# A two-layer convolution and feed-forward block: W_up moved to SyncE's queue, convolution 1 ahead of pair 3's first layer, eight weight sums moved to GpSimd

## The chip, the cores and the metric

One core of a Trainium2 chip runs the whole program once. Its engines are TensorE (PE, with PEld for its weight loads), VectorE (DVE), ScalarE (ACT), GpSimd (POOL) and SyncE (SP, which here only issues DMAs). Every engine works through its own instructions in the order in which the program has them, and waits on semaphores for the others. The metric is the device time of one launch in microseconds (us); the median over runs counts. All data is float32.

## The reference

`x` is 128 sequences of 64 channels and 1024 positions. Two layers follow each other, each a convolution-like step and then a matrix product over the 1024 positions, added to `x`:

```python
# layer 0: a 64x64 channel mix per sequence, chosen by attention over 8 kernels,
# then a product of rank 128
att   = softmax(gelu(gelu(cond @ W0 + b0) @ W1 + b1) @ W2 + b2)
agg_w = einsum('bk,koi->boi', att, weight)
out   = einsum('boi,bih->boh', agg_w, x) + (att @ bias_k)[:, :, None]
x     = x + einsum('bsd,od->bso', out, A @ B.T) + bias
# layer 1: a grouped convolution (4 groups, 9 taps), plus a context per sequence,
# then a full 1024x1024 product and a routed low-rank part
y     = conv1d(x, weight1, groups=4, padding=4) + (c @ c_weight.T)[:, :, None] + bias1[None, :, None]
delta = lora_B[e] @ (lora_A[e] @ y)         # e = argmax(gate_w @ y + expert_bias)
x     = x + y @ W_up.T + delta
```

## The kernel before

**Tiles.** Two sequences make a pair: 128 rows (two sequences of 64 channels) by 1024 positions, 0.5 MB. There are 64 pairs, numbered from 0. Two pairs make a step of the outer loop (L784), 32 steps in all. Constants such as W_up (4 MB, tile `w`), `at`, `bt`, `ws` stay in SBUF.

**Layer 0 of one pair** is three functions. `layer0_in` (L387) multiplies the turned x (`xt`) by B: 16 PE instructions into `pxb`, one ScalarE copy to `xb`. `layer0_mix` (L396) mixes channels with the pair's own 128x128 matrix into `pz`, and copies to `z`. The first four pairs (`FIRST = 4`) build that matrix on VectorE from their attention row (`own_bd`, L325, eight operations, tile `bdx`) and a bias on ScalarE (`own_bias`, L319, tile `mv`). Later pairs take it from DRAM, where `agg_all` and `agg_out` put all sequences' matrices (`aggd`, 2 MB), read back as `bd` and `ab` by `load_cond` (L232). `layer0_out` (L412) multiplies by A in two halves into `pd`; VectorE adds each half into `x` (L423), and SyncE writes it to a DRAM scratch `x1d` (L424) and reads it back in another layout as `X` (L431, L432), which waits until the write has landed. With `later=True` the two reads are returned as a function and issued where that is called. Before `layer0_out` the feed-forward bias must have been added to `x` (`add_fbias`, L646).

**Layer 1.** For the first two pairs (`PLAIN = 2`) the convolution `conv` (L524) multiplies `X` by `ws` directly: 64 PE instructions at L496 into `pc`; VectorE adds the context into `yt` (L517). Later pairs use differences of `X` built by GpSimd (`differences`, L451, tile `df`), a shared product `pm` (L467) added by VectorE (L482) and copied by ScalarE (L485), then L505 into `pc`, and L517.

**The 1024x1024 product** of a step is done as a fast block scheme: sums of quarters of `yt` (`Y_SUMS`, on GpSimd, `ffn_sums`, tiles `s`), sums of blocks of W_up (`W_SUMS`, once, `w_sums`), and 26 products of four PE instructions each (`PRODUCTS`, L549, into `pb`), whose results are added into place by VectorE and ScalarE. There are 31 entries in `W_SUMS`; each is one operation on 128x512 in the tile `w`. In `w_sums` ScalarE first copies one of the two operands to PSUM (`pw`, L197), and VectorE then adds (L206 or L204), except where an operand is one of the last two results, which is read from SBUF as it is. `gate_in`, `gate` and `turn` make the routed part's choice.

**The prologue** (L680 to L783) is ordered by hand over all five engines; every list below is in program order. SyncE: the loads of pairs 0 and 2, then for pairs 0 and 1 the writes and reads of `layer0_out`, with pair 3's loads (L705) between them, and pair 4's loads (L718) behind pair 1's reads; then the writes of pairs 2 and 3, their reads, the aggregated matrices, `load_cond(2)`, pair 5. ScalarE's queue: pair 1's loads and several constants, `gl` and `lb` (L715, L716), and the four quarters of W_up (L724, `load_w`, in the order 2, 1, 3, 0) between its own copies. The first 26 products come in `first_products` (L749), which before product i issues the sums that product i + 3 needs. The sums 0 to 2 are issued ahead of all products by `w_sums(3, False)`, with both operands in SBUF. DMAs issued by SyncE and ScalarE share eight completion semaphores taken in turn, so an issue can wait for the landing of the one eight places before it.

## Time and profile before

| | us |
|---|---|
| median of 3 runs | 1291.03 (1288.48 to 1291.08) |
| the profiled execution: its time | 1288.22 |
| its span | 1286.4 |
| PE busy in the span | 1259.9 (98%) |
| GpSimd / VectorE / ScalarE busy | 721.8 / 705.0 / 237.0 |
| first product (L549) starts | 57.8 |
| `pd` of pair 4 / of pair 5 starts | 80.3 / 87.1 |
| `pm` of pair 4 (L467) starts | 104.2 |
| X of pair 1: reads issued / landed | 33.4 and 34.2 / 47.5 and 49.2 |
| DMA over the span | 189.71 MB, mean 147 GB/s |

### The profile page before, as it was taken

How to read it: one execution, taken by the hardware profiler on the slowest of the kernel's cores; microseconds unless marked ns; L12 is line 12 of the kernel's file. 1: busy time of each engine (PE TensorE's matmuls, PEld its weight loads, DVE VectorE, ACT ScalarE, POOL GpSimd, SP SyncE). 2: the span in 40 equal slices, each digit the busy share in tenths (PEclk: the TensorE clock that was granted, in tenths of full speed). 3: DMA queues.
4: the chain of work that ended last, by engine and by line, in shares of the span. 5: the costliest groups of instructions: out<-in, count | busy, mean ns of one | idle time of the engine just before them, and what ended most of it. 6: DMA issues, size and time to landing. Idle time of an engine off the chain costs nothing.

```text
span 1286.4 us, 23722 instructions
## 1 busy us (share of the span) xinstructions
PE 1259.9 (98%) x9255; PEld 1059.1 (82%) x9255; DVE 705.0 (55%) x1484; ACT 237.0 (18%) x593; POOL 721.8 (56%) x861
## 2 busy tenths in 40 slices
PE   8789999999999999999999999999999999999998
PEld 6567888888888888888888888888888888888886
DVE  6586554555554565554565454565454565455454
ACT  2242112111112111111111111111111111111111
POOL 2345764556765546765556765546765555765432
PEclk9899999999999999999999999999999999999999
DMA  9954446544446544445654445654445654445301
GB/s 310 312 164 134 124 110 175 175 149 141 127 110 173 174 148 143 133 106 169 175 155 138 130 110 166 174 156 141 131 110 162 175 162 132 133 115 157 103 34 66
DMA packets 184158, 189.71 MB, mean 147 GB/s; under 512 B 17392, under 2 KB 156656, under 8 KB 183536
## 3 DMA queue, kind: packets, MB, share of 16 engines
q1 hardware_dynamic: 166192, 121.61, 34.7%
q0 software_dynamic: 16128, 58.73, 13.6%
q10 hardware_dynamic: 1728, 7.87, 1.7%
q8 instruction: 74, 1.21, 0.4%
q14 instruction: 36, 0.29, 0.1%
HBM read 118.90 MB, written 69.27 MB: 146 GB/s over the span
## 4 chain that ended last, share of the span: by engine, by line
PE 93%; DMA 3%; DVE 2%; issue 0%; ACT 0%; SPq 0%; DVEq 0%
PE pb L549 55%; PE pxb L391 9%; PE pd L422 8%; PE pc L505 8%; PE pm L467 5%; PE pg L576 4%; PE pb L622 3%; DMA X<-x1d 1%; PE pz L401 1%; DMA x<-in_x 1%; DVE yt L517 1%; DMA x1d<-x 1%; DMA xt<-in_xt 0%; PE pc L496 0%; DVE m L482 0%
## 5 line engine op out<-in xcount | busy, mean ns | idle before, releaser
L549 PE MATMUL pb<-w,s 128*128 128x256 f32 x2432 | 556.9, 380 | 1.8 <-DVE pb L554 0.9
L549 PEld LDWEIGHTS pb<-w,s 128*128 128x128 f32 x2432 | 459.9, 190 | 68.5 <-issue 1.7
L459 POOL TENSOR_TENSOR df<-X 128x512 f32<-128x512 f32 x62 | 64.3, 1037 | 390.8 <-DMA X<-x1d 362.3
L549 PE MATMUL pb<-w,yt 128*128 128x256 f32 x896 | 226.2, 381 | 2.6 <-DVE x L628 1.8
L482 DVE TENSOR_TENSOR m<-pm,cx 64x512 f32<-64x512 f32 x124 | 85.5, 689 | 201.7 <-PE pm L467 198.8
L549 PEld LDWEIGHTS pb<-w,yt 128*128 128x128 f32 x896 | 163.1, 191 | 31.8 <-issue 8.7
L566 DVE TENSOR_TENSOR x<-pb,x 128x256 f32<-128x256 f32 x320 | 129.1, 420 | 94.8 <-PE pb L549 88.1
L206 POOL TENSOR_TENSOR s<-yt,s 128x256 f32<-128x256 f32 x224 | 164.0, 732 | 17.8 <-PE pb L549 2.8
L647 POOL TENSOR_TENSOR x<-x,ffn_bias 128x1024 f32<-128x1024 f32 x62 | 144.8, 2352 | 42.0 <-DMA x<-in_x 42.0
L391 PEld LDWEIGHTS pxb<-B,xt 128*128 128x128 f32 x1024 | 118.8, 194 | 25.6 <-DVE yt L517 22.0
L517 DVE TENSOR_TENSOR yt<-pc,m 128x512 f32<-128x512 f32 x124 | 122.1, 1108 | 22.2 <-ACT m L485 20.0
L422 PE MATMUL pd<-AT,z 128*128 128x512 f32 x256 | 122.6, 601 | 3.4 <-DVE attx L317 1.3
L391 PE MATMUL pxb<-B,xt 128*128 128x128 f32 x1024 | 124.9, 280 | 1.0 <-PE pb L549 0.9
L505 PE MATMUL pc<-ws,df 128*64 128x128 f32 x1984 | 114.0, 273 | 1.2 <-DVE m L482 1.2
L423 DVE TENSOR_TENSOR x<-pd,x 128x512 f32<-128x512 f32 x128 | 88.3, 691 | 44.7 <-PE pd L422 38.1
L505 PEld LDWEIGHTS pc<-ws,df 128*64 128x64 f32 x1984 | 109.4, 137 | 1.6 <-POOL s L206 1.0
L561 ACT COPY v<-pb 128x256 f32<-128x256 f32 x96 | 35.8, 372 | 372.9 <-PE pb L549 355.4
L206 POOL TENSOR_TENSOR s<-s,yt 128x256 f32<-128x256 f32 x128 | 93.4, 730 | 14.9 <-PE pzt L613 7.5
L485 ACT COPY m<-m 64x512 f32<-64x512 f32 x124 | 76.6, 617 | 135.5 <-DVE m L482 125.7
L206 POOL TENSOR_TENSOR s<-s,s 128x256 f32<-128x256 f32 x128 | 92.7, 735 | 5.0
L568 DVE SCALAR_TENSOR_TENSOR x<-pb,x 128x256 f32<-128x256 f32 x128 | 54.0, 422 | 68.2 <-PE pb L549 66.6
L628 DVE TENSOR_TENSOR x<-pb,x 128x512 f32<-128x512 f32 x124 | 76.7, 681 | 8.7 <-PE pb L622 8.7
(107 smaller groups left out, 919.3 us busy)
## 6 DMA issues: line engine op xcount, KB each, us to landing
x1d<-x SPq DMA_DIRECT2D x128, 256.0 KB, 4.5
X<-x1d SPq DMA_DIRECT2D x128, 256.0 KB, 4.3
out<-x SPq DMA_DIRECT2D x62, 512.0 KB, 3.6
xt<-in_xt POOLq DMA_DIRECT2D x56, 512.0 KB, 5.8
x<-in_x POOLq DMA_DIRECT2D x56, 512.0 KB, 6.6
cx<-ctxd SPq DMA_DIRECT2D x32, 128.0 KB, 4.2
w<-in_wq ACTq DMA_DIRECT2D x4, 1024.0 KB, 7.7
ab<-aggbd SPq DMA_DIRECT2D x30, 128.0 KB, 3.3
```

What stands on the lines that cost most here:

```text
L206: eng.tensor_tensor(to, x, y, ALU.add if op == "+" else ALU.subtract)
L391: nc.tensor.matmul(pxb[:, :P], xt[:, c, :], bt[:, c, :], start=(c == 0), stop=(c == NC - 1))
L422: nc.tensor.matmul(pd, z0, at[:, cols], start=True, stop=True)
L423: nc.vector.tensor_tensor(x[:, cols], pd, x[:, cols], ALU.add)
L482: nc.vector.tensor_tensor(by_group(m2[half, b]), by_group(pm[half]), context(pr, b, half), ALU.add)
L485: nc.scalar.copy(m2[other, b], m2[half, b])
L505: nc.tensor.matmul(pc[o * H : (o + 1) * H, cols], diffs[pr][:, 2 * g + b, o], ws[:, g, o], start=True, stop=True,)
L517: nc.vector.tensor_tensor(yt.rearrange("m q (o g two) -> m two g q o", two=2, g=NGC)[:, b], by_group(pcs.pop((pr, b))), context(pr, b) if ...
L549: nc.tensor.matmul(p, ys[d][u][:, c], W[:, w, c], start=new == 1 and c == 0, stop=c == QC - 1, skip_group_check=True)
L566: nc.vector.tensor_tensor(x, p, x, ALU.add)
L628: nc.vector.tensor_tensor(x[:, cols], b, x[:, cols], ALU.add)
L647: eng.tensor_tensor(xs[pr], xs[pr], fbias, ALU.add)
```

## The change

Nothing of what is computed changes, except that eight sums are done on another engine. In the prologue:

- **W_up** is issued by SyncE instead of ScalarE, behind pair 1's two reads of X and pair 4's turned x. `load_x` is split in two, so that pair 4's turned x goes ahead of W_up and pair 4's x behind it and behind pair 2's writes. `lb` moves from ScalarE's queue to SyncE's, behind that. Pair 3's loads move from between pair 0's reads and pair 1's writes to between pair 1's writes and reads.
- **Convolution 1** moves from behind `layer0_out(3)` to between `layer0_in(3)` and `layer0_mix(3)`. `layer0_in(4)` moves from the middle of the first eight products to ahead of the gates and products.
- **Eight sums** (`ON_POOL`: 16, 19, 20, 21, 23, 24, 27, 28 of `W_SUMS`) are done by GpSimd from SBUF, without ScalarE's copy.
- **Biases**: pair 3's goes from GpSimd to VectorE, behind pair 2's output; pair 4's, on GpSimd, from ahead of the first sums of `yt` to behind the last.
- `own_bias` of pairs 2 and 3 goes up beside that of pair 1; of the products around `layer0_mix(4)` and (5), some change places with the mixes and `layer0_in(5)`.

```diff
 NW = 26
+ON_POOL = (16, 19, 20, 21, 23, 24, 27, 28)
...
+    def load_turned(pr, eng):
+        xts[pr] = xtp.tile([P, NC, P], F32, tag="xt", name=f"xt{pr}")
+        eng.dma_start(xts[pr], a["xt"][pr])
+
+    def load_rest(pr, eng):
+        xs[pr] = xpool.tile([P, L], F32, tag="x", name=f"x{pr}")
+        eng.dma_start(xs[pr], a["x"][pr])
+
     def load_x(pr, eng=nc.gpsimd):
...
+        load_turned(pr, eng)
+        load_rest(pr, eng)
...
             first = W[:, x]
+            if k in ON_POOL:
+                combine(nc.gpsimd, W[:, to], first, op, W[:, y])
+                continue
             if aside and x not in fresh:
...
-    own_bias(1)
+    for pr in range(1, FIRST):
+        own_bias(pr)
     load_context(0)
     layer0_out(0)
 
-    load_x(3, nc.sync)
     add_fbias(1, nc.vector)
...
     gl = loaded("gl", [P, NC, GT], eng=nc.scalar)
-    lb = loaded("lb", [P, N], eng=nc.scalar)
-    layer0_out(1)
-    load_x(4, nc.sync)
+    back1 = layer0_out(1, later=True)
+    load_x(3, nc.sync)
+    back1()
+    load_turned(4, nc.sync)
+    for k in (2, 1, 3, 0):
+        load_w(k, nc.sync)
     wsum = const.tile([P, NGC, P], F32, tag="sel", name="wsum")
     nc.gpsimd.tensor_tensor(wsum, ws[:, :, 0], ws[:, :, 1], ALU.add)
-    add_fbias(3, nc.gpsimd)
     next(agg)
-    for k in (2, 1, 3, 0):
-        load_w(k, nc.scalar)
     own_bd(2)
-    own_bias(2)
     layer0_in(2)
     own_bd(3)
-    own_bias(3)
     conv(0)
     layer0_mix(2)
     back2 = layer0_out(2, later=True)
+    load_rest(4, nc.sync)
+    lb = loaded("lb", [P, N], eng=nc.sync)
+    add_fbias(3, nc.vector)
     layer0_in(3)
+    conv(1)
     layer0_mix(3)
     back3 = layer0_out(3, later=True)
     back2()
...
     w_sums(3, False)
-    conv(1)
+    layer0_in(4)
 
     gate_out(0, gate_in(0))
-    add_fbias(4, nc.gpsimd)
     ffn_sums(0, 0, 10)
...
-    first_products(4)
-    layer0_in(4)
-    first_products(4)
+    first_products(8)
     differences(2)
     differences(3)
     ffn_sums(0, 10)
+    add_fbias(4, nc.gpsimd)
     add_fbias(5, nc.gpsimd)
...
-    first_products(4)
+    first_products(3)
     layer0_mix(4)
+    first_products(1)
     layer0_out(4, lambda: load_x(6, nc.sync))
-    first_products(2)
     layer0_in(5)
+    first_products(1)
     layer0_mix(5)
+    first_products(1)
     layer0_out(5, lambda: load_x(7, nc.sync))
```

More of the change, by code (lines that the diff above doesn't have):

```diff
@@ L152, in block @@
     xs, xts, bds, aggbs, ctxs = {}, {}, {}, {}, {}
+    def load_turned(pr, eng):
[4 more added lines that the diff above has]
+        eng.dma_start(xs[pr], a["x"][pr])
     def load_x(pr, eng=nc.gpsimd):
-        xts[pr] = xtp.tile([P, NC, P], F32, tag="xt", name=f"xt{pr}")
-        xs[pr] = xpool.tile([P, L], F32, tag="x", name=f"x{pr}")
-        eng.dma_start(xts[pr], a["xt"][pr])
-        eng.dma_start(xs[pr], a["x"][pr])
+        load_turned(pr, eng)
+        load_rest(pr, eng)
     BD = []
```

## The prediction

> **What bounds the kernel now.** I read the stage table first, to see where TensorE is not full; then the chain of waits in the stage where it is not; then the DMA queues in the wait that the chain names; then the timeline of GpSimd and VectorE, since work moves between them. Pairs are counted from 0.

> In the stage table the columns are the stretch, its length, then busy time (and instructions) of PE, PEld, DVE, ACT and POOL, the granted clock, the DMA share and GB/s:

> ```profile
> 0.00:29.00 29.00, 23.66 (x127) 16.90 (x127) 18.63 (x46) 8.67 (x22) 6.54 (x20) 0.94 0.91 305
> 29.00:58.00 29.00, 20.36 (x193) 15.86 (x194) 14.87 (x23) 2.14 (x9) 6.71 (x5) 0.88 0.99 305
> 58.00:68.00 10.00, 9.14 (x52) 7.71 (x53) 8.10 (x14) 7.39 (x17) 9.53 (x13) 1.00 0.72 243
> 68.00:80.00 12.00, 9.83 (x114) 8.28 (x110) 11.81 (x20) 4.24 (x7) 7.57 (x8) 1.00 0.34 100
> 80.00:104.00 24.00, 20.76 (x84) 15.00 (x84) 17.50 (x36) 9.29 (x20) 10.75 (x9) 0.93 0.73 189
> 104.00:1286.00 1182.00, 1176.17 (x8692) 995.32 (x8690) 634.05 (x1348) 205.26 (x519) 680.66 (x809) 1.00 0.48 139
> ```

> From 104 us on, PE is busy 1176 of 1182 us: whatever brings that point forward ends the kernel earlier by as much. The change touches only what lies before it. Of 29 to 58 us PE works 20.4, with the DMA engines full (0.99). From 58 to 104 PE works 39.7 of 46, and VectorE is the fullest engine from 68 to 80 (11.8 of 12).

> The chain of waits between 20 and 60 us (start, length, what):

> ```profile
> 27.54 6.64 DMA x1d<-x
> ...
> 34.19 15.02 DMA X<-x1d
> ...
> 49.35 5.40 PE pc L496 x64
> ...
> 55.90 1.96 PE pg L576 x30
> ```

> Convolution 1 (L496) waits for pair 1's X, whose read takes 15.02 us; pair 0's took 5.6. The DMA view of 34 to 44 us says why:

> ```profile
> q10 hardware_dynamic: 471, 3.46, 94.3%
> q1 hardware_dynamic: 283, 0.14, 5.3%
> ```

> q10 is ScalarE's queue, on which W_up (4 MB) was issued from 31.0 us; q1 is SyncE's, with X. X moves 0.14 MB in 10 us beside W_up's 3.46.

> VectorE and GpSimd in the timeline (start, length):

> ```profile
> 30.72 4.64 DVE L332 SCALAR_TENSOR_TENSOR bdx<-wk,attx,bdx 128x128 f32<-128x128 f32 x7
> ...
> 32.40 2.42 POOL L647 TENSOR_TENSOR x<-x,ffn_bias 128x1024 f32<-128x1024 f32 x1 [8.53 <-DMA x<-in_x]
> ```

> The same seven VectorE operations took 2.68 us without GpSimd beside them: 1.96 more for GpSimd's 2.42. And later GpSimd stands idle for 16.4 us:

> ```profile
> 92.56 1.04 POOL L459 TENSOR_TENSOR df<-X 128x512 f32<-128x512 f32 x1 [16.44 <-PE pb L549]
> ```

> **W_up behind X.** Pair 1's sums are ready at 24.70 and 25.93 (L423); SyncE issues their writes then, no longer behind pair 3's loads. A write and a read take 4.5 + 4.3 at the page's medians, 6.6 + 5.6 in the loaded stretch: X is there between 34.8 and 38.2, not at 49.2. W_up follows in the queue behind pair 3's 1 MB, X and pair 4's turned x, from about 36. At q10's 3.46 MB in 10 us its 4.19 MB take 12.1: the last quarter lands near 49, 2 us later than before (47.1). The first sum that needs it is W_SUMS[3].

> **TensorE to product 0.** ScalarE no longer issues W_up, where it stood 7.2 us ahead of the copy that mix(2) waits for. Convolution 0 at 29.4, as before, takes 3.7: 33.1. Mix 2 x 0.49, copy 0.3, output 2.0: 36.4. L391 for pair 3, 2.0: 38.4. Convolution 1 (X is there by either bound), 3.7 by convolution 0's row; its own 5.4 came at a granted clock of 0.70 after an idle stretch that is gone: 42.1. Mix, copy and output of pair 3, 3.3: 45.3. L391 for pair 4 2.0, gates L576 1.9: product 0 at 49.2 against 57.8. VectorE keeps up: without pair 3's bias on GpSimd its second row of seven ends at 33.3, not 35.4. It takes that bias itself (1.23, the row at 12.9 us) at 37.2, ahead of the convolution's first half at 40.2; were pair 3's x to land after 39, the cover would be gone and all 1.23 would count. The four ScalarE activations moved up (0.29 each, 1.2) lie in its 3.05 us gap before 19.3; lb's issue moves to SyncE, where it costs 0.8 of waiting time.

> What is late next is VectorE: W_SUMS 0 to 2 now meet GpSimd's sums (0.73 each, from 43), which came after them before. Each 0.69 waits between 0 and 0.73; I take all: 46.1 + 4.3 = 50.4 when sum 3 starts, against 58.7. **Gain so far 8.3.** [...]

> **To the convolutions of pairs 2 and 3.** Sum 3 to L482 took 58.7 to 70.8, VectorE nearly without a gap. L391 for pair 4 (2.0 on PE) leaves it, but VectorE sets the pace: between 0 and 2.0, I take 0.5. X of pairs 2 and 3 must be there by 61. Their writes now queue behind W_up (to 48), then pair 4's x and lb (0.75 MB, 1.9 at the 400 GB/s of a full stretch): X lands near 55 and 58, hidden by 3 us.

> **The eight sums.** Each leaves VectorE (0.69) and ScalarE (0.59, its copy to PSUM) and costs GpSimd 1.04 by the row at 92.56 (same shape), or 2.12 by L720's, which ran against VectorE. I take 1.04, as VectorE's other sums read PSUM copies: 8.3 us inside an idle 16.4. Sum 16 stands behind bias 5, which waits for pair 5's x. Behind the sums wait differences 4, biases 6 and 7, differences 5: 74.7 + 8.3 + 2.1 + 4.7 + 2.1 = 91.9, wanted by L505 at 95.6, hidden by 3.7.
> From L482 to pd of pair 4: 9.6 before, one sum less: 0.6. From there to L467 at 104.2: 23.9 before. PE's own work in it is 14 products at 0.865 (chain: 16 matmuls 3.46), two outputs 3.5, L391 2.0, mix and wait 1.3, transposes 0.3: 19.2. So 4.7 at most, and nothing at least, if VectorE's dependent steps stay. Seven of the eight sums leave here (4.8 of VectorE's 17.5), so PE becomes the bound: I take 4.6.

> **Sum** 8.3 + 0.5 + 0.6 + 4.6 = 14.0. The profiled execution took 1288.2 (span 1286.4): 1274.2. The runs shown lie 0.3 to 2.9 above it, median 2.8; I add half: **1275.5**. The ends: no lock (0.8), X of pair 0 1 us sooner since lb is out of its way, 1.5 more in the second stage: 17.3, and 18 with the range's rounding; without the last stage 9.4.

> **Rivals.**
> A: *the aggregation's DMA chain becomes the bound.* The same bytes go through engines that were full to 64 us. From pair 3's last write (50.3) the chain ran 15.2 to agg, 4.9 to ab, 3.3 to pair 5's x (73.7). New it starts at 46.2 with 3 us of transfers ahead: ab near 69, x near 72.5, needed at 69.7 and 72.6. For: no slack. Against: only the excess counts. If nothing lands sooner than before, mix(4) waits 0.7 and sum 16 is up to 3 late: gain 10.5, 1279.
> B: *GpSimd at 2.12 a sum:* 17 us, differences 5 end 5 late: gain 9, 1280.5. Against: VectorE has few operations with two SBUF tiles there.
> C: *moving W_up does nothing for X,* which lands at 45 to 49 anyway, and pair 3's layer 0 stands behind a late convolution. For: the same bytes, full engines. Against: the 0.14 MB. Convolution 1 at 45.5 to 49.3 instead of 38.4 takes 7 to 11 of the 14: 1282 to 1287. [...]
> D, *slower: SyncE's head blocks.* X's reads wait on SyncE for the write's landing, and now W_up, the next writes and the aggregation stand behind them. Each us that X is late past 38.4 moves convolution 1 and W_up alike: even at 52.4, slower by over 0.2% from 55; at 58, 1294. For: SyncE stood 9.2 us ahead of pair 2's write, for a read of X that this write did not need. Against: it takes 29 us from write to read, and the 6.6 + 15.0 was with W_up on another queue.
> E: *no effect*, 1288 to 1291: only if PE's idle returned elsewhere in full.

> **Chances.** Forecast 0.62, A 0.15, B 0.06, C 0.09, D 0.05, E 0.03. The range runs from 18 of gain (1270) over A and B to the middle of C: 1270 to 1284. A measurement here tells 0.2% (2.6 us) from no change. Faster: all but D, E and the end of C, 0.91; same 0.04; slower 0.05.

> **What would show it.** Pair 1's X landing before 38.4, W_up's last near 49; convolution 1 before mix(3), from about 38; product 0 near 49; sums on GpSimd near 1.04, in a row from about 75; pair 4's first L467 near 90; the rest 1182 long. Wrong: X after 45, mix(4) waiting for ab, product 13 for GpSimd, or over 30 us from product 0 to pd of pair 5.

## The result, and the profile after

| | before | after |
|---|---|---|
| median on the same chips, 5 runs each | 1288.48 us (1284.06 to 1291.08) | 1278.93 us (1277.43 to 1279.74) |
| ratio of the means, 95% interval | | 0.9935 (0.9915 to 0.9954) |
| the profiled execution: time, span | 1288.22, 1286.4 | 1279.21, 1277.4 |

Faster by 0.65%: 9.0 us in the profiled spans, where the forecast had 14.0. Functions lie ten lines further down in the changed kernel: L496 is now L506, L549 L559, L423 L433, L424 L434, L467 L477, L482 L492, L595 L605, L647 L657. Points of the two traces beside the forecast, in us:

| | before | forecast | after |
|---|---|---|---|
| pair 1's X landed (two reads) | 47.5, 49.2 | 34.8 to 38.2 | 34.4, 36.0 |
| W_up's last quarter landed | 47.1 | 49 | 47.6 |
| convolution 1 starts | 49.4 | 38.4 | 37.2 |
| product 0 starts | 57.8 | 49.2 | 47.8 |
| first L482 (now L492) | 70.8 | 62.0 | 60.7 |
| `ab` landed; pair 5's x landed | 70.4; 73.7 | 69; 72.5 | 69.4; 72.0 |
| `pd` of pair 4 | 80.3 | 70.9 | 69.9 |
| `pm` of pair 4 | 104.2 | 90.2 | 95.5 |
| from there to the end | 1182.2 | 1182 | 1181.9 |

Up to pair 4's `pd` the change gave 10.4 us, 1.0 more than forecast (9.4). From there to pair 4's `pm` it lost: that stage took 23.9 before, 19.3 was forecast, and it takes 25.5. So 14.0 + 1.0 - 6.2 + 0.3 (the rest) gives the 9.0 within rounding. The stage table of the changed kernel shows the same; its columns are those of the table shown before:

```profile
29.00:48.00 19.00, 18.01 (x199) 14.37 (x194) 14.74 (x24) 1.18 (x5) 5.47 (x7) 1.00 1.05 362
48.00:60.00 12.00, 10.32 (x86) 8.41 (x87) 10.34 (x18) 7.08 (x16) 7.75 (x9) 1.00 1.05 310
60.00:70.00 10.00, 7.15 (x65) 5.60 (x61) 9.33 (x17) 3.06 (x5) 6.90 (x8) 1.00 0.48 156
70.00:95.50 25.50, 20.46 (x86) 15.21 (x86) 16.30 (x28) 5.93 (x14) 23.06 (x19) 0.93 0.77 186
95.50:1277.00 1181.50, 1175.90 (x8691) 995.32 (x8690) 634.75 (x1348) 205.16 (x519) 679.25 (x808) 1.00 0.48 139
```

In the first row PE works 18.0 of 19 us, where it worked 20.4 of 29 before product 0. In the fourth it works 20.5 of 25.5 at a granted clock of 0.93, while GpSimd, which had 10.8 of 24 there, is busy for 23.1. PE has slack in that stage, VectorE too (16.3), so neither is full: some chain of dependent steps sets its length.

**The first gain.** The chain of waits, in which the read of X held convolution 1 for 15 us, now passes there from PE's work to PE's work:

```profile
35.50 1.78 PE pxb L401 x16
37.29 3.65 PE pc L506 x64
40.94 0.42 PE pz L411 x2
41.35 0.43 PE pz L416 x2
42.19 2.00 PE pd L432 x4
```

and in the DMA view of 34 to 44 us one queue is left, which moves 3.93 MB where the two moved 3.6:

```profile
q1 hardware_dynamic: 653, 3.93, 101.1%
```

**The loss.** The timelines of VectorE, of GpSimd and of PE in the last stage (start, length):

```profile
85.50 1.00 DVE L605 TENSOR_TENSOR sc<-lg,mx 128x8 f32<-128x8 f32 x1
86.53 2.27 DVE L606 TENSOR_TENSOR sc<-sc,rank 128x8 f32<-128x8 f32 x1
88.84 0.16 DVE L608 TENSOR_REDUCE ms<-sc 128x2 f32<-128x8 f32 x1
89.03 2.07 DVE L610 TENSOR_TENSOR oh<-sc,ms 128x8 f32<-128x8 f32 x1
91.14 0.36 DVE L613 TENSOR_TENSOR zm<-pgt,oh 128x64 f32<-128x64 f32 x2
```

```profile
74.36 10.13 POOL L216 TENSOR_TENSOR w<-w 128x512 f32<-128x512 f32 x8
84.43 1.05 POOL L469 TENSOR_TENSOR df<-X 128x512 f32<-128x512 f32 x1
85.43 1.05 POOL L470 TENSOR_TENSOR df<-X 128x512 f32<-128x512 f32 x1
86.42 4.66 POOL L657 TENSOR_TENSOR x<-x,ffn_bias 128x1024 f32<-128x1024 f32 x2
```

```profile
86.22 1.89 PE L559 MATMUL pb<-w,s 128*128 128x256 f32 x8
91.55 0.46 PE L623 MATMUL pzt<-ident,zm 128*128 128x128 f32 x1 [3.44 <-DVE zm L613]
92.14 2.07 PE L559 MATMUL pb<-w,s 128*128 128x256 f32 x4
94.01 1.53 PE L559 MATMUL pb<-w,yt 128*128 128x256 f32 x4
95.47 1.98 PE L477 MATMUL pm<-wsum,X 128*64 128x128 f32 x32
```

L605, L606 and L610 are three of the gate's steps on 8 numbers a row; L608, of the same size, takes 0.16. Each of the three has two operands in SBUF, and each ends with a GpSimd instruction: the second difference at 86.48, the first bias at 88.75 (half of the pair), the second at 91.08. PE needs the gate's answer `zm` for a transpose (L623), which stands ahead of the last two products in its order, and idles for 3.44. Its last eight product matmuls then take 3.60, and the windows view says why (first the idle stretch, then these):

```profile
88.00:91.60 3.60, 0.16 (x2) 0.06 (x1) 3.50 (x6) 0.00 (x0) 3.60 (x3) 1.00 0.73 106
91.60:95.00 3.40, 3.27 (x8) 2.43 (x9) 1.09 (x2) 0.27 (x1) 3.24 (x5) 0.50 0.00 0
```

The granted clock is 0.50 from 91.6 to 95.0, right behind the gap. The theory to be tested: the eight sums, 10.1 us on GpSimd, put differences 4 and the biases of pairs 6 and 7 on top of the gate, whose tiny two-SBUF steps (1.00, 2.27 and 2.07) each end only with a GpSimd instruction, and PE loses the wait (3.44) and then half its clock (0.50).

### The profile page after: what moved, and what is told of

Read it like the earlier page. It is cut to its first block, busy times and chain, and to the rows that moved or that the text cites. A ratio compares the mean times of both kernels' runs of the same rounds, so it can differ in the third digit from the quotient of the medians.

```text
span 1277.4 us, 23722 instructions
## 1 busy us (share of the span) xinstructions
PE 1257.3 (98%) x9255; PEld 1057.8 (83%) x9255; DVE 704.5 (55%) x1477; ACT 232.3 (18%) x585; POOL 728.5 (57%) x868
## 3 DMA queue, kind: packets, MB, share of 16 engines
q10 hardware_dynamic: 1008, 3.41, 0.8%
## 4 chain that ended last, share of the span: by engine, by line
PE 95%; DVE 2%; POOL 1%; DMA 1%; issue 1%; ACT 0%; ACTq 0%; POOLq 0%; DVEq 0%
PE pb L559 55%; PE pxb L401 9%; PE pd L432 9%; PE pc L515 8%; PE pm L477 4%; PE pg L586 4%; PE pb L632 3%; PE pz L411 1%; DMA x1d<-x 1%; POOL s L216 0%; DVE bdx L342 0%; POOL x L657 0%; DMA X<-x1d 0%; DVE yt L527 0%; PE pc L506 0%
## 5 line engine op out<-in xcount | busy, mean ns | idle before, releaser
L559 PE MATMUL pb<-w,s 128*128 128x256 f32 x2432 | 557.1, 380 | 3.0 <-DVE x L576 1.7
L559 PEld LDWEIGHTS pb<-w,s 128*128 128x128 f32 x2432 | 459.5, 190 | 68.7 <-issue 3.3
L559 PE MATMUL pb<-w,yt 128*128 128x256 f32 x896 | 226.1, 381 | 2.4 <-DVE x L638 1.8
L492 DVE TENSOR_TENSOR m<-pm,cx 64x512 f32<-64x512 f32 x124 | 85.4, 689 | 203.1 <-PE pm L477 200.2
L559 PEld LDWEIGHTS pb<-w,yt 128*128 128x128 f32 x896 | 163.3, 191 | 32.2 <-issue 8.7
L576 DVE TENSOR_TENSOR x<-pb,x 128x256 f32<-128x256 f32 x320 | 129.2, 421 | 95.0 <-PE pb L559 88.4
L657 POOL TENSOR_TENSOR x<-x,ffn_bias 128x1024 f32<-128x1024 f32 x61 | 142.2, 2347 | 21.3 <-DMA x<-in_x 21.3
L527 DVE TENSOR_TENSOR yt<-pc,m 128x512 f32<-128x512 f32 x124 | 122.7, 1110 | 22.4 <-ACT m L495 21.5
L433 DVE TENSOR_TENSOR x<-pd,x 128x512 f32<-128x512 f32 x128 | 88.4, 692 | 38.3 <-PE pd L432 31.5
```

Of the source, the lines that this page charges most:

```text
L433: nc.vector.tensor_tensor(x[:, cols], pd, x[:, cols], ALU.add)
L492: nc.vector.tensor_tensor(by_group(m2[half, b]), by_group(pm[half]), context(pr, b, half), ALU.add)
L527: nc.vector.tensor_tensor(yt.rearrange("m q (o g two) -> m two g q o", two=2, g=NGC)[:, b], by_group(pcs.pop((pr, b))), context(pr, b) if ...
L559: nc.tensor.matmul(p, ys[d][u][:, c], W[:, w, c], start=new == 1 and c == 0, stop=c == QC - 1, skip_group_check=True)
L576: nc.vector.tensor_tensor(x, p, x, ALU.add)
L657: eng.tensor_tensor(xs[pr], xs[pr], fbias, ALU.add)
```

## The experiments

### e1: the gate's small tiles in PSUM

The logits `lg` and scores `sc` go into free columns of the PSUM tile `pt` in which the gate's transpose already stands. Each of the three steps then has one SBUF operand; order and engines stay.

```diff
-        lg = sp.tile([P, 2, E], F32, tag="lg", name=f"lg{d}")
+        lg = pt[:, P : P + 2 * E].rearrange("p (t e) -> p t e", t=2)
...
-        sc = sp.tile([P, 2, E], F32, tag="sc", name=f"sc{d}")
+        sc = pt[:, P + 2 * E : P + 4 * E].rearrange("p (t e) -> p t e", t=2)
```

> The changed kernel, with the gate's small tiles lg and sc put into unused columns of the PSUM bank that its transpose already holds, so that no VectorE step of the gate has two SBUF inputs; nothing else moves. Theory L (the missing 5 us are VectorE's gate steps standing behind GpSimd's differences 4 and biases 6 and 7, and the half-clock stretch after TensorE's idle): the steps at 85.5 to 91.1 (1.00, 2.27 and 2.07 us) fall to about 0.2 each, the transpose pzt waits under 0.5 instead of 3.44, no half-clock stretch follows, and the first pm of pair 4 starts at 90 to 91 instead of 95.5; span about 1272.5. Rival Q (the gate is late because VectorE's own queue is full or the steps wait for their inputs): the steps stay near 1 to 2 us, pm at 95 and the span at 1277.

Median 1273.22 us (4 runs, 1272.77 to 1273.44), ratio to before 0.9888 (0.9872 to 0.9905), below the change's whole interval. VectorE, GpSimd and PE of its timeline:

```profile
85.16 0.17 DVE L605 TENSOR_TENSOR pgt<-pgt,mx 128x8 f32<-128x8 f32 x1
85.37 0.17 DVE L606 TENSOR_TENSOR pgt<-pgt,rank 128x8 f32<-128x8 f32 x1
...
85.78 0.17 DVE L610 TENSOR_TENSOR oh<-pgt,ms 128x8 f32<-128x8 f32 x1
```

```profile
85.09 1.04 POOL L470 TENSOR_TENSOR df<-X 128x512 f32<-128x512 f32 x1
86.08 4.69 POOL L657 TENSOR_TENSOR x<-x,ffn_bias 128x1024 f32<-128x1024 f32 x2
```

```profile
87.60 0.27 PE L623 MATMUL pzt<-ident,zm 128*128 128x128 f32 x1
87.71 1.03 PE L559 MATMUL pb<-w,s 128*128 128x256 f32 x4
88.57 1.03 PE L559 MATMUL pb<-w,yt 128*128 128x256 f32 x4
89.53 1.97 PE L477 MATMUL pm<-wsum,X 128*64 128x128 f32 x32
```

All three steps take 0.17 beside GpSimd's second difference (85.09 to 86.13), and are over before the biases begin. PE doesn't wait at the transpose and keeps its clock (1.00 from 70 to 89.5). `pm` starts at 89.53 instead of 95.47. By PE's lines of both kernels the 5.94 us are made up of 0.35 by which PE is earlier at the row of 86.22, 3.60 up to the transpose (the wait), 0.48 to the product behind it, and 1.51 in the two products at half clock. Pair 4's `pd` lies at 69.65 here, so the stage takes 19.9, against 19.3 of the forecast.

So the same step took 2.27 with both operands in SBUF and 0.17 with one of them in PSUM. What sets the half clock off isn't shown: in the change 0.50 came behind an idle 3.44, and in the kernel before at 36.18, behind a wait of 2.25, but there also at 97.62, where PE's last two waits had been 0.90 and 0.85, while in the change the clock stayed at 1.00 behind one of 1.68 (at 55.13).

### e2: the biases of pairs 6 and 7 behind differences 5

The same theory from GpSimd's side: the gate stays as it is, and in the first step of the loop the two long GpSimd instructions come after the second pair's differences instead of the first's.

```diff
-        for pr, plus in zip((2 * d + 4, 2 * d + 5), (ahead, ())):
+        for pr, plus in zip((2 * d + 4, 2 * d + 5), (ahead, ()) if d else ((), ahead)):
```

> The changed kernel, with GpSimd's biases 6 and 7 moved behind differences 5 in the first step alone; the gate stays as it is. Theory L: the gate meets only differences 4 (one step of about 1 us), its end comes at 87 to 88, pzt waits under 0.5, the first pm of pair 4 starts at 90 to 91; GpSimd's sums of step 1 start near 98 instead of 93, which the products of step 1 still allow, so the span is about 1272.5. Rival Q: the gate's steps stay long, pm at 95, span 1277. If GpSimd's later sums become the bound instead, pm is at 91 but the span stays at 1275 or above, with products of step 1 waiting for sums.

Median 1274.32 us (4 runs, 1272.61 to 1274.81), ratio 0.9893 (0.9872 to 0.9914). On VectorE:

```profile
86.50 1.00 DVE L605 TENSOR_TENSOR sc<-lg,mx 128x8 f32<-128x8 f32 x1
87.54 0.17 DVE L606 TENSOR_TENSOR sc<-sc,rank 128x8 f32<-128x8 f32 x1
```

Only L605 is still held, by a difference (1.00). In this run the DMAs of the first stages came about 1.1 us later (pair 4's `pd` at 71.0), so the stage counts: 20.1 instead of 25.5, `pm` at 91.07. GpSimd does the biases from 92.8 and is 4.5 us later at the sums of `yt` for step 1 (97.5 instead of 93.0); from `pm` to the end it still took 1181.9. Nothing was given back there.

### e3: without the eight sums on GpSimd

```diff
-ON_POOL = (16, 19, 20, 21, 23, 24, 27, 28)
+ON_POOL = ()
```

> The changed kernel without the eight sums on GpSimd: all 31 are back on VectorE with ScalarE's copies; W_up's queue, the order of the convolutions and the biases stay as changed. The prediction's term (the eight sums are worth 4.6 in the last stage and 0.6 before it): pm of pair 4 at 100 to 101, span about 1282.5. Theory L (the sums pushed GpSimd's biases into the gate, which took most of that back): without them the biases run before most of the gate, and the loss is smaller than 4.6: pm at 96 to 98, span 1278 to 1280.

Median 1279.13 us (4 runs, 1278.85 to 1280.03), ratio 0.9936 (0.9919 to 0.9953): the change's own ratio. As it stands in the change, moving the sums gained nothing that these runs can tell. `pm` starts at 94.83, sooner than even the leading theory had it. VectorE and PE:

```profile
86.55 2.24 DVE L606 TENSOR_TENSOR sc<-sc,rank 128x8 f32<-128x8 f32 x1
...
89.48 2.67 DVE L216 TENSOR_TENSOR w<-pw,w 128x512 f32<-128x512 f32 x4
```

```profile
90.31 2.05 PE L559 MATMUL pb<-w,s 128*128 128x256 f32 x4 [2.22 <-DVE w L216]
```

GpSimd's biases start at 84.1 without the sums and meet one gate step instead of three. But VectorE has the sums behind the gate in its order (the row of four from 89.48), and PE waits 2.22 for one of them. That wait is the gate's again, passed on by the sum: in e8, where the same sums stand behind a gate that nothing holds up, the same product waits 0.18. The product behind the wait is slow here too: its row of four at 90.31 takes 2.05, where the one at 87.06 takes 1.03. So the chain gate, sum, PE costs here about what the chain gate, transpose, PE costs in the change.

### e4: W_up back on ScalarE's queue

All else as in the change.

```diff
-    for k in (2, 1, 3, 0):
-        load_w(k, nc.sync)
...
     next(agg)
+    for k in (2, 1, 3, 0):
+        load_w(k, nc.scalar)
     own_bd(2)
```

> The changed kernel with W_up's four loads issued by ScalarE again, at their old place behind the second part of the aggregation; everything else stays as changed. [...] Rival Q2 (it was only the order of issue that mattered, here X ahead of W_up in time): X lands at 34 to 37 as in the changed kernel, and product 0 moves by less than 2.

One run, 1284.66 us, span 1282.9. The reads of X landed at 40.0 and 47.2. Its DMA view of 34 to 44 us, and its chain of waits:

```profile
q10 hardware_dynamic: 346, 2.50, 70.9%
q1 hardware_dynamic: 970, 0.94, 33.3%
```

```profile
25.96 8.90 DMA x1d<-x
...
34.87 12.34 DMA X<-x1d
...
47.35 5.35 PE pc L506 x64
```

X is slow again beside W_up in another queue: 10.7 and 12.3 us for the two reads instead of 5.2 and 6.2, and 8.9 for the write. Convolution 1 costs 5.35 behind the idle stretch (2.47), as before (5.40). X's order of issue doesn't explain it: the first read was issued at 29.4, as in the change (29.2), and the second at 34.87, level with W_up's third quarter (34.88) and ahead of the fourth (36.0), and still it landed only at 47.2. So it is the queue, not X's earlier issue, that brought X forward. Product 0 starts at 59.55, 11.8 later than in the change (rival Q2 had less than 2), since convolution 1 now stands ahead of pair 3's mix, and the first stages wait behind it. The end is only 5.5 later: the gate comes later too and meets one of GpSimd's biases instead of a difference and two biases (L605 takes 2.15, the other two steps 0.17), and PE waits 0.59 for it (`pm` at 101.0).

### e5: convolution 1 back behind pair 3's output

```diff
     layer0_in(3)
-    conv(1)
     layer0_mix(3)
...
     w_sums(3, False)
+    conv(1)
     layer0_in(4)
```

> The changed kernel with convolution 1 back behind pair 3's output and sums 0 to 2; W_up stays on SyncE and the eight sums on GpSimd. Theory (X is there by 36, so the place of the convolution only decides what VectorE and GpSimd can begin): product 0 at 48 to 50, L482 1 to 3 us later than 60.7, because the sums of yt start about 4 us later; span 1278 to 1280. Rival (the place is what gave the gain): product 0 at 52 or later.

One run, 1281.09 us, span 1279.3. Product 0 starts at 48.9 (1.1 later), L492 at 61.5 (0.8 later), `pm` at 96.25 (0.8 later). The other 1.1 of the 1.9 in the span came behind `pm`; the run's mean granted clock was 0.997, the change's 0.998. By this one run, its place is worth about one microsecond, with X early.

### e6: the kernel before, with the gate in PSUM

The edit of e1 made to the kernel before.

```diff
-        lg = sp.tile([P, 2, E], F32, tag="lg", name=f"lg{d}")
+        lg = pt[:, P : P + 2 * E].rearrange("p (t e) -> p t e", t=2)
...
-        sc = sp.tile([P, 2, E], F32, tag="sc", name=f"sc{d}")
+        sc = pt[:, P + 2 * E : P + 4 * E].rearrange("p (t e) -> p t e", t=2)
```

> The kernel before, with only the gate's tiles in PSUM. Theory L: the one long gate step there (1.77 us at 97.5, beside GpSimd's bias 7) falls to 0.2, pm of pair 4 starts 1 to 3 us sooner than 104.2, and the half-clock stretch at 97.6 may stay or go. Rival: no change of the steps.

One run, 1287.88 us, span 1286.1. On VectorE, where the kernel before has 1.77 for the same step:

```profile
98.74 0.17 DVE L595 TENSOR_TENSOR pgt<-pgt,mx 128x8 f32<-128x8 f32 x1
```

The run's mean granted clock was 0.997, that of the kernel before in its profile 0.994. There the half-clock stretch (97.62 to 101.03, at 0.50) began with the long step (97.51), ahead of any wait that the step could cause, so these runs don't show what set it off. The stage from pair 4's `pd` to its `pm` takes 22.35 instead of 23.9, but `pd` itself came 1.2 later in this run with its DMAs, so the span hides it. The gate's trouble was in the kernel before, for about 1.6 us, the excess of that one step, behind which a sum and then PE waited; in the change it costs 5.6 (e1's 5.94 without the 0.35 that lie ahead of it).

### e7: e1, nine sums moved, and pair 4's x and `lb` behind the aggregation

An attempt at a faster one: sums 11 and 12 go to GpSimd instead of 16, so that product 13 doesn't wait, and the aggregation's chain has fewer bytes ahead of it. The edits beside those of e1:

```diff
-ON_POOL = (16, 19, 20, 21, 23, 24, 27, 28)
+ON_POOL = (11, 12, 19, 20, 21, 23, 24, 27, 28)
...
-    load_rest(4, nc.sync)
-    lb = loaded("lb", [P, N], eng=nc.sync)
     add_fbias(3, nc.vector)
...
     agg_out()
+    load_rest(4, nc.sync)
+    lb = loaded("lb", [P, N], eng=nc.sync)
     load_cond(2)
```

> The changed kernel with the gate's tiles in PSUM as in the first experiment, two more early sums (11 and 12) on GpSimd, where it stands idle for 4 us before differences 2, sum 16 back on VectorE, and pair 4's x and lb issued behind the aggregation's writes instead of ahead of them. Theory: VectorE reaches L482 about 1.3 us sooner (59.3 against 60.6), the aggregation's ab lands about 1.9 sooner (67.2 against 69.1), product 13 no longer waits 0.8 for GpSimd, and pm of pair 4 starts near 87 against 89.5; span about 1269. Rival (the aggregation's chain is fixed by its own latencies, not by what is queued ahead): ab lands at 69 again and takes back what VectorE gains, pm at 89, span 1271.

Median 1272.89 us (4 runs, 1272.49 to 1272.99), ratio 0.989 (0.9869 to 0.9911). Its interval covers e1's: both beat the change, and they can't be told from each other. L492 at 59.4 came as expected, and `pm` of pair 4 at 88.16 is 1.4 sooner than e1's. `ab` landed at 68.4, only 0.7 sooner than e1's 69.1 and not 1.9. Most of the 1.4 was given back at once, so the span is the rival's 1271, though not by the rival's wait for `ab` alone:

```profile
90.03 1.10 PE L477 MATMUL pm<-wsum,X 128*64 128x128 f32 x16 [0.77 <-DMA X<-x1d]
```

PE is now ahead of pair 5's X: past e1, the next wait in this place is one for a transfer.

### e8: e1 without the eight sums on GpSimd

The two lines of e1, and:

```diff
-ON_POOL = (16, 19, 20, 21, 23, 24, 27, 28)
+ON_POOL = ()
```

> The first experiment's kernel (gate in PSUM) without the eight sums on GpSimd. Now that the gate no longer meets GpSimd, this prices the eight sums themselves. The prediction's term: 4.6 in the last stage, 0.6 before: pm of pair 4 near 94.5 instead of 89.5, span 1276.5. Rival (VectorE had room for most of them): pm at 90 to 92, span 1272 to 1274.

Median 1276.38 us (4 runs, 1275.62 to 1276.69), ratio 0.9916 (0.989 to 0.9941): 3.2 behind e1 by the medians, though the intervals overlap a little. In the profiled run W_up's last quarter landed at 49.8 instead of 47.6 and pair 4's `pd` came 1.5 later; the stage from there takes 21.5 against e1's 19.9. The product that waited 2.22 in e3:

```profile
89.44 1.10 PE L559 MATMUL pb<-w,s 128*128 128x256 f32 x4 [0.18 <-DVE w L216]
```

So with the gate out of the way the eight sums are worth 1.6 us in that stage, by one profiled run of each; whether the other 1.5 is the run or the edit, these runs don't say.

### e9: the kernel before, with W_up alone moved

W_up's four loads on SyncE behind pair 4's loads, nothing else.

```diff
     load_x(4, nc.sync)
+    for k in (2, 1, 3, 0):
+        load_w(k, nc.sync)
...
-    for k in (2, 1, 3, 0):
-        load_w(k, nc.scalar)
```

> The kernel before with one edit: W_up's four loads are issued by SyncE, behind pair 4's two loads, instead of by ScalarE. No other order changes, no sum moves. Theory Q1 (X starves beside W_up on another queue): X of pair 1 lands near 38 instead of 47.5 and 49.2; convolution 1, which here stands behind pair 3's layer 0 and sums 0 to 2, starts when those are done, near 44 to 47 instead of 49.4, W_up's last quarter lands near 50 instead of 47, and the first pm of pair 4 starts 2 to 5 us before 104.2. Rival (the queue only matters together with the new order of the convolutions): X lands early, but pm of pair 4 moves by less than 1.

Median 1284.83 us (10 runs, 1280.99 to 1287.2) beside 1287.76 of the kernel before (13 runs); ratio 0.998 (0.9964 to 0.9996). X landed at 36.4 and 37.5, W_up at 51.4. PE:

```profile
44.42 3.72 PE L496 MATMUL pc<-ws,X 128*64 128x128 f32 x64
...
51.20 1.13 PE L549 MATMUL pb<-w,yt 128*128 128x256 f32 x4
```

Convolution 1 starts without a wait and takes 3.72, not 5.40; product 0 comes 6.6 sooner, `pm` 6.0 sooner in this run, which is at the fast end of the ten. By the medians the edit is worth 2.9 us. Which of the two is nearer isn't settled: these runs spread over 6 us.

## Why the prediction was right, and where it failed

**Right: faster, and inside the range of 1270 to 1284.** The forecast of 1275.5 is 3.4 below the measured 1278.93: 5.0 less gain in the span, and 1.6 back from the term that stood for the median, since the changed kernel's median lies 0.3 under its profiled execution and not 1.3 above it. That the time is inside the range was in part luck: the last stage fell outside its own bounds, and the range had room for that only because it was drawn over rivals A (1279) and B (a gain of 9). By the number alone either of them would look right, yet neither's mechanism took what was lost.

**W_up behind X: right.** X landed inside the forecast's bounds or just ahead of them, W_up 1.4 sooner than forecast, the convolution at full clock in 3.72. Rival C fell: e9 moves W_up alone, and X lands at 36.4 and 37.5; e4 puts W_up back on its own queue, and X's second read lands at 47.2. The two arrangements, e4's and the change's, differ by 11 us for that read. Rival D fell with it: SyncE blocked nothing that was needed, with X there by 36.0.

**TensorE to product 0 and on to pair 4's `pd`: right, 1.0 better.** Sum 3 began 10.0 sooner than before (8.3 forecast); the two terms behind it gave 0.1 to L492 (0.5) and 0.3 to `pd` (0.6). Most of the surplus came from a place that the sum took "as before": convolution 0 began at 28.13 and not at 29.4, since pair 0's X landed at 27.5 instead of 29.2 and PE did not wait for it (1.15 before). The forecast had that among the ends of its range, put down to `lb`'s move, which no run tested. Sums 0 to 2 on VectorE took 3.25, not 4.3; of the 2.2 us of waiting for GpSimd's sums that the forecast took in full, 1.15 came (the three took 2.10 before). The 0.8 that the range has for "no lock" (sums that wait for nothing on GpSimd) was the author's estimate, and no run shows it: in the change these three sums meet GpSimd's and last this long:

```profile
44.81 2.14 DVE L216 TENSOR_TENSOR w<-w 128x512 f32<-128x512 f32 x2
46.99 1.11 DVE L214 SCALAR_TENSOR_TENSOR w<-w 128x512 f32<-128x512 f32 x1
```

**Rival A: there, but small.** `ab` and pair 5's x landed within 0.5 us of where the forecast put them. Pair 4's mix waited 0.55 for `ab`, and product 13 waited 0.90 for sum 16, which stands behind pair 5's bias.

**The eight sums: the step that failed.** The prediction said: "Seven of the eight sums leave here (4.8 of VectorE's 17.5), so PE becomes the bound: I take 4.6." PE did not become the bound. The stage got 1.6 longer instead of 4.6 shorter, outside its own bounds of "4.7 at most, and nothing at least". Two things were mis-sized or missed in it:

- A sum costs GpSimd 1.27 (10.13 for eight), not 1.04. The row of the same shape was too cheap a stand-in. Rival B's 2.12 was too dear, and its mechanism (differences 5 late) didn't decide: GpSimd was late for the gate first.
- The lower bound held only "if VectorE's dependent steps stay". They didn't. The prediction asked what is queued behind the sums on GpSimd (differences 4, biases 6 and 7) and when their results are wanted, and found 3.7 us of slack. It didn't ask which VectorE steps would run at the same time as they. And against rival B it argued that "VectorE has few operations with two SBUF tiles there": few, but the gate's are in a row, and PE waits for the last. By the forecast's own times they could have been found: sums to 83, differences 4 to 85.1, biases to 89.8, and the gate, at 97.5 before, 10 to 14 us sooner.

e1, with the operands' place changed and nothing else, gives the stage its 19.9; e2 shows the same from the other engine. With the gate free the stage is 4.05 shorter than before (23.93 to 19.88), close to the 4.6, but the sums are less than half of that: about 1.6 are the gate's own (e6) and 1.6 the sums' (e8). The other 0.85 lie between e6's stage (22.35) and e8's (21.5), so in the change's remaining moves or in the runs. As the change stands, e3 says that its third part, the sums, is worth nothing; the rest carries it. What that rest is made of is only partly shown: without the sums the change gains 8.6 by the medians (e3), W_up alone 2.9 (e9), and the convolution's place about 1 (e5). What is missing lies in the other moves of the prologue, in how they act together, or in the spread of the runs; no run separates these.

The simplest version that beats both kernels is e1's: 0.9888 of the time before, two lines beyond the change.

## What to carry to other kernels

When work is moved to another engine, lay the whole queue behind it on the time axis, and look not only at who waits for its results but at which dependent chain on the neighbouring engine has two SBUF operands in the same microseconds. Here the smallest operations were hit hardest: three gate steps, 0.17 without GpSimd's delay, took 1.00, 2.27 and 2.07, each until a GpSimd instruction ended, while sums 0 to 2 together went from 2.10 to 3.25. An operand in PSUM took that chain out of reach, without a change of order (0.17 a step beside GpSimd's difference, e1). And a large load that several things want later belonged here in the queue behind a transfer that was wanted now (X there by 36.0), not beside it in another queue (47.2 in e4).

## What the runs showed of the hardware that was not expected

- A VectorE step on 128x8 with two SBUF operands took 2.27 us beside a GpSimd instruction of 2.33, where it takes 0.17 alone (e2, at 87.54, GpSimd's difference over at 87.48). Each of the held steps ended with the GpSimd instruction beside it (88.80 and 88.75, 91.10 and 91.08).
- A GpSimd sum of two 128x512 blocks within `w` takes 1.27, the differences of two 128x512 blocks of `X` 1.04. The cause wasn't tried.
- Two queues did not share evenly by bytes: beside W_up in its own queue X's got 0.94 MB in 10 us with 970 packets (e4), W_up's 2.50 MB with 346; in one queue, 3.93 MB in all, X landed at 34.4 and 36.0 and W_up's quarters behind it at 39.5, 42.7, 45.2 and 47.6.
- Each half-clock stretch named here lasted 3.41 us: in the kernel before from 36.18 and from 97.62, in the change from 91.59.
- The runs of e1 and e7 spread over 0.7 and 0.5 us, those of the kernel before over 5 to 7. What makes the spread wasn't tested.
